# Two-layer convolution and attention kernel: order of first-image loads, idle matrix products, product order in q's first tile, and dealing of the sampling steps

## The chip, the cores and the metric

The kernel runs on one core of a Trainium2 chip, in one launch. The core has five engines that run their own instruction streams side by side: TensorE (PE; its weight loads are listed as PEld), VectorE (DVE), ScalarE (ACT), GpSimd (POOL) and SyncE (SP). They wait for each other through semaphores. Transfers between the chip's main memory and the on-chip buffers are issued here by SP's and POOL's queues and carried by 16 DMA engines. Matrix products are written to PSUM, a small memory of banks that DVE and ACT can read. The metric is device time in microseconds (us); the median of several runs counts.

## What is computed

Input x has 8 images of 512 channels and 64x64 pixels, in 32-bit floats. Two layers are added to it:

```
x = x + L0(group_norm(x))      # deformable attention
x = x + L1(group_norm(x))      # 1x1 conv, depthwise stride 2, two dense layers, depthwise deconv, 1x1 conv
```

Layer 0, cut to what matters here:

```
q    = w_q @ x                               # 512x512 times 512x4096, per image
t    = gelu(q[every 4th row and column] * w_off1 + b_off1)
off  = tanh(w_off2 @ t) * 4                  # 16x16 sampling points for each of 8 groups
kv_feats = bilinear_sample(q, grid + off)    # four neighbours of each point, weighted
k, v = split(w_kv @ kv_feats)
out  = softmax(q^T k / 8) v                  # 8 heads, 4096 queries, 256 keys
y    = w_out @ out + b_out
```

Group norm needs mean and variance of groups of 16 channels over the whole image, so no product of an image can begin before all of the image has been read and its statistic is done.

## The kernel before, in words

**Staging.** Images are worked one after the other. x of two images is held on chip. An image is 8 tiles (t = 0 to 7) of 512 pixels, each 128 partitions x 4 channel blocks x 512. All instructions stand in the order in which the code issues them (the schedule is by hand); each engine and each DMA queue keeps its own order.

**The first image.** At the top of the program two small arrays are loaded, `cst` (L114: the matrix that sums over groups, and constants of the sampling) and `vec` (L116: biases and small weights). Both stand on SP's queue ahead of `load_x(0)` (L1060, eight loads of 1 MB), `load_wq()` (the weights of q, in `wbuf`), `load_x(1)` and later weights. `norm_x` (L201) takes a statistic of each tile and channel block on DVE as it lands. `group_stats` joins them (L169), sums over groups with a product with `cst` (L173, tile `gps`), forms squared deviations on DVE, does a second such product (L182, `gpsb`), adds epsilon (L184) and takes the power -1/2 on POOL (L185). `norm_q` then normalises tile 0 on DVE and tile 1 on POOL (L217, four channel blocks each); later tiles are normalised on ACT (L221).

**q's seven products.** `project_q` computes a tile of q by a Winograd-Strassen scheme: seven products of quarter matrices instead of eight. `of_weights` and `of_tile` form the sums of weights (s1, s2, s4) and of pixels (t1, t2) on DVE: L253, L255, L257, L259 and L264, L266, L268, L270. `product` (L275) issues four matrix products of 128x128 by 128x256 in 32-bit floats; a trace shows two records for each, so a product is 8 records. In a tile, PE's order is: products 1 and 2, then 6 (s2, t2), 7, 5 (s1, t1), 4, 3. DVE adds them up as they come:

```
q12 = q11 + p6   (L364)      q11 += p2   (L365)      q22 = q12 + p7   (L372)
q12 += p5        (L378)      q21 = q22 + p4 (L385)   q22 += p5 (L386)   q12 += p3 (L391)
```

In tile 0, s4 is formed (L259) between L365 and L372, for all images but image 1, whose weights' sums are still there from image 0. Products 1 and 2 share a two-bank PSUM tile, and so do 7 and 4; products 6, 5 and 3 take single banks from a pool of two (`ps_mm`). From tile 1 on, transposes of the tile before (`by_pixel`, L324) stand between the products; tile 0 has none.

**Steps and dealing.** `project_q` is a generator; it yields a number for the PE work issued: 4, 2.5, 2.5, 2.5, 2.5 and 2 for the six parts of a tile, 16 together. `sample` is a generator too: it forms the sampling positions (three yields of 0), then goes through 20 slots (yield None). In them DVE computes row numbers (L516), POOL gathers q's pixels from main memory (L519), DVE weighs them (L483 to L488) and, twice, PE transposes the result (L493) into a bank of `ps_mm`, from where ACT copies it (L498). The sampling of image 0 is dealt among the q products of image 1 by the loop at L1087: each slot adds 6 units of room, and q steps are issued until the room is used up. When the slots are done, the rest of image 1's q follows. For later images other loops do this. Then `project_k` (L533) and `project_v` (L560) make k and v, and attention rounds begin, in which the next images' loads, statistics, q and layer 1 of the image before are mixed.

Of the kernel before, what the change touches and what calls it, by code (L numbers as in the profile page):

```python
# [8 lines left out]
F32 = mybir.dt.float32  # L9
# [7 lines left out]
P = 128  # L17
# [5 lines left out]
TP = 512  # L23
NT = N // TP
# [25 lines left out]
def kernel(  # L50
# [15 lines left out]
    nc = tc.nc  # L66
# [8 lines left out]
    ps_a = ctx.enter_context(tc.tile_pool(name="ps_a", bufs=1, space=PSUM))  # L75
# [20 lines left out]
    def spot(b, k):  # L96
        j = region[b]
        k %= NT + 1
        return spares[j] if k == 0 else regions[j][:, :, (k - 1) * TP : k * TP]

    def x_tile(b, t):
        return spot(b, t + 1)

    def q_tile(b, t):
        return spot(b, t)
# [5 lines left out]
    ident = cpool.tile([P, P], F32, name="ident")  # L111
    make_identity(nc, ident)
    cst = cpool.tile([P, K_N], F32, name="cst")
    nc.sync.dma_start(cst, consts)  # L114
    vec = cpool.tile([P, V_N], F32, name="vec")
    nc.sync.dma_start(vec, vecs)  # L116
    nhalf = cpool.tile([P, NCC], F32, name="nhalf")
    nc.vector.memset(nhalf, -0.5)

# [14 lines left out]
    def load_wq():  # L134
        nc.sync.dma_start(wbuf, w_qT.rearrange("(cc p) o -> p cc o", p=P))
# [19 lines left out]
    def drain(*gens):  # L155
        for gen in gens:
            for _ in gen:
                pass
# [35 lines left out]
    def load_x(b, order=range(NT), queue=nc.sync):  # L194
        for t in order:
            queue.dma_start(x_tile(b, t), xs[place[b]][:, :, t * TP : (t + 1) * TP])
# [7 lines left out]
    def quarters(a):  # L204

        h = C // 2
        return [[a[:, 2 * i : 2 * i + 2, h * j : h * (j + 1)] for j in range(2)] for i in range(2)]
# [25 lines left out]
    def project_q(b, normalise, mq, qd, pools, sums, aside=None):  # L233
# [8 lines left out]
        s1, s2, s4, t1, t2_, first = sums  # L242
# [29 lines left out]
        def product(bank, w, xh):  # L272
            for o in range(2):
                for k in range(2):
                    nc.tensor.matmul(  # L275
                        bank[:, o * 2 * P : (o + 1) * 2 * P],
                        w[:, k, o * P : (o + 1) * P],
                        xh[:, k, :],
                        start=(k == 0),
                        stop=(k == 1),  # L280
                    )
            return bank.rearrange("p (o n) -> p o n", o=2)
# [25 lines left out]
        def one_bank(t, n):  # L308
            return ps_mm.tile([P, TP], F32, tag="mm", name=f"pq_{b}_{t}_{n}")
# [33 lines left out]
        for t in range(NT):  # L343
            (x11, x12), (x21, x22) = quarters(x_tile(b, t))
            (q11, q12), (q21, q22) = quarters(q_tile(b, t))

            def pixels(k):

                if t:
                    by_pixel(t - 1, k)  # L350
                if t + 2 < NT:
                    normalise(t + 2, k)

            bank1, bank2 = two_banks(t, 0)
            p1 = product(bank1, w11, x11)
            p2 = product(bank2, w12, x21)
            nc.scalar.copy(q11, p1)
            of_tile(t, 4)
            if t:
                activate(t - 1)  # L360
            yield 4
            p6 = product(one_bank(t, 1), s2, t2_)
            pixels(0)
            V.tensor_add(q12, q11, p6)  # L364
            V.tensor_add(q11, q11, p2)  # L365
            if t == 0:
                of_weights(4)
            yield 2.5
            bank1, bank2 = two_banks(t, 2)
            p7 = product(bank1, w21, x12)  # L370
            pixels(1)
            V.tensor_add(q22, q12, p7)  # L372
            if aside and t in (3, 4):
                largest(2, t - 3)
            yield 2.5
            p5 = product(one_bank(t, 3), s1, t1)
            pixels(2)
            V.tensor_add(q12, q12, p5)  # L378
            if t + 1 < NT:
                of_tile(t + 1, 1)  # L380
                of_tile(t + 1, 2)
            yield 2.5
            p4 = product(bank2, w22, x21)
            pixels(3)
            V.tensor_add(q21, q22, p4)  # L385
            V.tensor_add(q22, q22, p5)  # L386
            if t + 1 < NT:
                of_tile(t + 1, 3)
            yield 2.5
            p3 = product(one_bank(t, 4), s4, x22)  # L390
            V.tensor_add(q12, q12, p3)  # L391
            if t == 2 and aside:
                aside()
            elif t + 1 < NT:
                largest(t, 0)
                largest(t, 1)
            yield 2
# [660 lines left out]

    with tc.manual_schedule():
        load_x(0)  # L1060
        load_wq()
        load_x(1)

        wkv = [es4[0:2], es4[2:4]]
        for i in range(2):
            for j in range(2):
                w = w_kvT.rearrange("(cc p) o -> p cc o", p=P)
                nc.sync.dma_start(wkv[i][j], w[:, 2 * j : 2 * j + 2, i * C : (i + 1) * C])
        load_weights_late()
        st = new_stats(0, 0)  # L1070
        drain(norm_x(0, st))

        shared = [wout[:, i, :].rearrange("p (k o) -> p k o", k=2) for i in range(3)]
        shared += [kt[:, 0:2, :], kt[:, 2:4, :], wout[:, 3, :]]
        drain(norm_q(0, st, norms))

        st = new_stats(0, 1)
        blocks, other = norm_x(1, st), norm_q(1, st, norms)
        for n, step in enumerate(make_q(0, shared)):
            if n >= 3 * NCC and next(blocks, "end") == "end" and n >= 10 * NCC:  # L1080
                next(other, None)
        drain(other)
        other = make_q(1, shared)
        next(other)
        rest.pop(0)()
        room = 0
        for step in samples[0]:  # L1087
            room += 6 if step is None else 2
            while room > 0:
                room -= next(other, 6) or 6  # L1090
        drain(other)
        rest.pop(1)()
        next(samples[1])
        load_wout()
        project_k(0, mqs.pop(0), wkv[0])
        logits(*names[0])
        project_v(0, wkv[1])
        for g in range(len(names) + LAG):
            b, r = divmod(g, ROUNDS)
            if r == 0 and b < B:  # L1100
                beside = next_image(b)
                st1s[b] = new_stats(1, b)

            def fill(room):
                while room > 0:
                    done = next(beside, None)
                    if done is None:
                        break
                    room -= done

            summed = g % 2 == 0 and 0 <= g - 1 < len(names)
            if g % 2 == 0:
                scale_two()
            if g < len(names):
                weighted_values(*names[g])
            if summed:
                sum_exps(*names[g - 1])
            if g < len(names):
                add_exps(*names[g])
            if r == Q_ROUND and 0 < b < B - 1:  # L1120

                tiles = [free_es.pop(0) for _ in range(3)]
                made = make_q(b + 1, room_for_sums(tiles), lambda: invert(*names[g - 1]))
                while next(made) != LATE:
                    pass
                free_es.extend(tiles)
                logits(*names[g + 1])
                drain(made)
                rest.pop(b + 1)()
            else:  # L1130
                if summed:
                    invert(*names[g - 1])
                if g + 1 < len(names):
                    logits(*names[g + 1])
            if g % 2:
                scale_two()
            phase[0] = 0
            if r >= LAG:
                fill(200)
            if g - LAG >= 0:  # L1140
                ob, ot, oc = names[g - LAG]
                project_out(ob, ot, oc, st1s[ob])
            k = g + 1 - LAG
            if 0 <= k < len(names) and k % NCC < 2:
                load_residual(*names[k + k % NCC], 2)
            if k >= NCC and k % NCC == 2 and names[k - NCC][0] < B - 1:
                store(*names[k - NCC][:2])
            phase[0] = 1
            if r >= LAG - 1:
                fill(200)  # L1150
            if b + 1 < B:
                if r == ROUNDS - 2:
                    drain(beside)
                    project_k(b + 1, mqs.pop(b + 1))
                if r == ROUNDS - 1:
                    project_v(b + 1)
        drain(layer1_last(B - 1, st1s.pop(B - 1), B - 2))
# [118 lines left out]
```

## Time and profile before

| | |
|---|---|
| median of 4 runs | 3288.21 us (3287.39 to 3289.61) |
| profiled execution | 3290.05 us |
| its span, first to last instruction | 3288.3 us |
| mean granted TensorE clock | 0.991 |
| DMA | 390.62 MB, mean 119 GB/s |

| line, engine | what | count | ns of one |
|---|---|---|---|
| L275 PE | products of q, 128x256 | 3584 records | 379 (median) |
| L560 PE | v, 128x512 | 16 in image 0 | 7.06 us from 283.89 on |
| L201 DVE | statistic of a block | 256 | 678 |
| L519 POOL | gather | 256 | 1109 |
| L217 DVE | normalise a block of tile 0, image 0 | 4 | 736 |

How to read it: the span counts from the first to the last instruction; the run's own time has some 1.8 us around it. A PE record's duration contains the filling of the array, so records overlap; the distance between starts says how fast PE works. A line of the timeline gives the start, the time to the end of the group, the engine, the line of the code, the operation, the tile written and those read, the shape, the count, and in brackets the idle time of that engine before it with what ended it.

### The profile page before, as it was taken

To read this page: it belongs to the slowest core of one execution; us is meant where nothing else is said; L and a number is where in the kernel's file an instruction comes from. 1 tells how busy PE (TensorE), PEld (TensorE's weight loads), DVE (VectorE), ACT (ScalarE), POOL (GpSimd) and SP (SyncE) were. 2 spreads that over 40 slices of the span, in tenths; PEclk is the share of its full clock that TensorE was granted. 3 is DMA by queue.
4 is the path that set the end of the run, shared out by engine and by line. 5 is a ranking of instruction groups with operands and counts; after the bars stand their busy time and mean duration, and the time that the engine had idled before them with its cause. 6 is when DMAs were issued, how large, how long until landed. Compare 5 with 4: busy or idle time off the path is not lost.

```text
span 3288.3 us, 46198 instructions
## 1 busy us (share of the span) xinstructions
PE 3207.1 (98%) x18196; PEld 1531.4 (47%) x18196; DVE 2330.1 (71%) x3786; ACT 1185.6 (36%) x1641; POOL 615.9 (19%) x576
## 2 busy tenths in 40 slices
PE   6999999999999999999999999999999999999996
PEld 5884223348332583326733276332853338533222
DVE  7884765787757777587765977668776687757565
ACT  2343333344323433344333443324432344333420
POOL 1130400130402304022030221303121040310201
PEclk9999999999999999999999999999999999999996
DMA  7232222672326623285332843248232582322713
GB/s 275 77 92 76 77 78 65 196 157 74 113 91 212 126 86 105 78 233 114 102 101 101 211 102 110 83 149 202 74 103 87 183 179 66 121 73 74 133 41 128
DMA packets 293874, 390.62 MB, mean 119 GB/s; under 512 B 18320, under 2 KB 157840, under 8 KB 293648
## 3 DMA queue, kind: packets, MB, share of 16 engines
q1 hardware_dynamic: 240368, 261.72, 24.4%
q0 software_dynamic: 53280, 125.86, 17.2%
q8 instruction: 145, 2.38, 0.3%
q14 instruction: 81, 0.66, 0.1%
HBM read 193.52 MB, written 192.94 MB: 118 GB/s over the span
## 4 chain that ended last, share of the span: by engine, by line
PE 93%; DVE 4%; issue 1%; ACT 1%; DMA 0%; SPq 0%; POOL 0%; ACTq 0%; DVEq 0%; POOLq 0%
PE pp L667 27%; PE pq L275 23%; PE ps L580 14%; PE pa L598 13%; PE pqt L324 4%; PE pn L625 4%; PE pk L533 2%; PE py L750 2%; PE pv L560 2%; PE po L893 2%; DVE rn L638 1%; PE po L424 0%; DVE st L201 0%; PE pu L848 0%; PE po_s L893 0%
## 5 line engine op out<-in xcount | busy, mean ns | idle before, releaser
L667 PE MATMUL pp<-image,wout 128*64 128x512 f32 x3584 | 820.2, 599 | 4.8 <-DVE image L653 4.6
L588 ACT ACTIVATE es<-ps 128x1024 f32<-128x1024 f32 x512 | 502.8, 1023 | 258.0 <-PE ps L580 208.7
L667 PEld LDWEIGHTS pp<-image,wout 128*64 128x64 f32 x3584 | 237.3, 137 | 549.7 <-issue 468.3
L598 PE MATMUL pa<-es,vt 128*64 128x512 f32 x2048 | 489.2, 598 | 1.7 <-ACT es L588 1.7
L519 POOL DMA_INDIRECT g<-qd,row x256 | 284.0, 1109 | 1053.9 <-DVE row L516 988.3
L275 PE MATMUL pq<-image,wbuf 128*128 128x256 f32 x2048 | 476.7, 381 | 3.3 <-DVE image L217 1.9
L580 PE MATMUL ps<-image,kt 64*64 64x512 f32 x3584 | 437.4, 602 | 0.3
L275 PEld LDWEIGHTS pq<-image,wbuf 128*128 128x128 f32 x2048 | 382.1, 191 | 56.2 <-issue 5.0
L674 DVE SCALAR_TENSOR_TENSOR image<-pp,vec,image 128x512 f32<-128x512 f32 x224 | 167.1, 746 | 335.9 <-PE pp L667 335.6
L605 ACT COPY image<-pa 128x512 f32<-128x512 f32 x224 | 132.1, 590 | 675.1 <-PE pa L598 675.1
L610 DVE TENSOR_TENSOR es<-es,es 128x1024 f32<-128x1024 f32 x256 | 310.8, 1214 | 71.4 <-PE pa L598 71.4
L598 PEld LDWEIGHTS pa<-es,vt 128*64 128x64 f32 x2048 | 137.4, 137 | 294.6 <-issue 274.8
L580 PEld LDWEIGHTS ps<-image,kt 64*64 64x64 f32 x3584 | 114.4, 132 | 307.7 <-issue 175.7
L638 DVE RECIPROCAL rn<-pn 128x512 f32<-128x512 f32 x64 | 214.6, 3353 | 7.7 <-PE pn L625 5.9
L334 ACT COPY qr<-pqt 128x512 f32<-128x512 f32 x224 | 131.2, 586 | 238.4 <-PE pqt L324 225.3
L185 POOL TENSOR_TENSOR gs<-ve,nhalf 128x4 f32<-128x4 f32 x16 | 16.7, 1042 | 1022.0 <-DVE ve L184 1022.0
L651 DVE STREAM_SHUFFLE rb<-rn 128x512 f32<-128x512 f32 x256 | 187.3, 732 | 0.1
L275 PE MATMUL pq<-es,es 128*128 128x256 f32 x768 | 181.5, 379 | 0.0
L945 POOL DMA_DIRECT2D out_dram<-part x126 | 138.1, 1323 | 153.8 <-ACT part L940 146.5
L201 DVE BATCH_NORM_STATS2 st<-image 128x6 f32<-128x512 f32 x256 | 159.2, 678 | 7.5 <-DMA image<-in_x_dram 7.4
L677 DVE BATCH_NORM_STATS2 st<-image 128x6 f32<-128x512 f32 x224 | 155.6, 694 | 7.7
L653 DVE TENSOR_TENSOR image<-image,rb 128x512 f32<-128x512 f32 x224 | 155.0, 692 | 7.8
(197 smaller groups left out, 3491.4 us busy)
## 6 DMA issues: line engine op xcount, KB each, us to landing
qd<-qr SPq DMA_DIRECT2D x256, 256.0 KB
image<-in_x_dram SPq DMA_DIRECT2D x112, 512.0 KB
out_dram<-image SPq DMA_DIRECT2D x49, 1024.0 KB
image<-in_x_dram POOLq DMA_DIRECT2D x48, 1024.0 KB, 10.6
out_dram<-part POOLq DMA_DIRECT2D x126, 256.0 KB, 7.1
image<-in_x_dram SPq DMA_DIRECT2D x16, 1024.0 KB
wbuf<-in_w_kvT_dram SPq DMA_DIRECT2D x14, 1024.0 KB
out_dram<-spare POOLq DMA_DIRECT2D x56, 256.0 KB, 8.0
```

What stands on the lines that cost most here:

```text
L201: nc.vector.bn_stats(st[:, cc, t, :], x_tile(b, t)[:, cc, :])
L275: nc.tensor.matmul(bank[:, o * 2 * P : (o + 1) * 2 * P], w[:, k, o * P : (o + 1) * P], xh[:, k, :], start=(k == 0), stop=(k == 1),)
L519: nc.gpsimd.indirect_dma_start(held[-1][:, i, :, :].rearrange("p j d -> p (j d)"), None, qd[:, :], bass.IndirectOffsetOnAxis(ap=row[:, ky, ...
L580: nc.tensor.matmul(ps[k : k + DH, a, :], kt[r : r + DH, hp, kc * P + k : kc * P + k + DH], qt[r : r + DH, hp, :], start=True, stop=True,)
L588: nc.scalar.activation(e, ps, AF.Exp)
L598: nc.tensor.matmul(pa[a * DH : (a + 1) * DH, :], vt[:, kc, hd * DH : (hd + 1) * DH], es[kc][:, a, :], start=(kc == 0), stop=(kc == 1),)
L610: nc.vector.tensor_add(es[0], es[0], es[1])
L638: nc.vector.reciprocal(rn, denominators.pop((b, t)))
L651: nc.vector.stream_shuffle(rb, rn, [2 * (hp % 2) + hp // 2] * 32)
L667: nc.tensor.matmul(pp[r : r + DH, :], wout[:, hp, oc * P + r : oc * P + r + DH], ao[:, hp, :], start=(hp == 0), stop=(hp == NCC - 1),)
L674: nc.vector.scalar_tensor_tensor(xt[:, oc, :], pp, col(V_BOUT + oc), xt[:, oc, :], ALU.add, ALU.add)
L677: nc.vector.bn_stats(st[:, oc, t, :], xt[:, oc, :])
```

## The change

Four edits:

- `cst` and `vec` are issued after `load_x(0)` instead of at the top.
- Five matrix products whose result nobody reads, of the unit matrix with 512 pixels of x's tile 6, are put between the statistic's DVE work and its first sum over groups; two more between its second sum and the first product of q. They write a PSUM bank that is first used later.
- In tile 0 of every image, product 5 is issued before product 6, third after 1 and 2. The additions keep their order.
- In the loop that deals image 0's sampling among image 1's q, a slot adds 4.5 units of room instead of 6.

```diff
@@ top
     cst = cpool.tile([P, K_N], F32, name="cst")
-    nc.sync.dma_start(cst, consts)
     vec = cpool.tile([P, V_N], F32, name="vec")
-    nc.sync.dma_start(vec, vecs)
@@ project_q, in the loop over tiles
             yield 4
+            if t == 0:
+                p5 = product(one_bank(t, 3), s1, t1)
             p6 = product(one_bank(t, 1), s2, t2_)
             pixels(0)
             V.tensor_add(q12, q11, p6)
@@
             yield 2.5
-            p5 = product(one_bank(t, 3), s1, t1)
+            if t:
+                p5 = product(one_bank(t, 3), s1, t1)
             pixels(2)
             V.tensor_add(q12, q12, p5)
@@ main part
         load_x(0)
+        nc.sync.dma_start(cst, consts)
+        nc.sync.dma_start(vec, vecs)
         load_wq()
         load_x(1)
@@
+        idle = ps_a.tile([P, TP], F32, tag="pa", name="idle")
+        for _ in range(5):
+            nc.tensor.matmul(idle, ident, x_tile(0, NT - 2)[:, 0, :], start=True, stop=True)
         drain(norm_q(0, st, norms))
+        for _ in range(2):
+            nc.tensor.matmul(idle, ident, x_tile(0, NT - 2)[:, 0, :], start=True, stop=True)
@@
         for step in samples[0]:
-            room += 6 if step is None else 2
+            room += 4.5 if step is None else 2
```

The code has the idle products of the second group after `drain(norm_q(...))`, so in PE's stream they stand between `gpsb` and the first product of q.

## The prediction

> **What bounds the kernel now.** I read the page's first part, then a table of stages made with the windows view, then the timeline of the first 50 us, of images 1 and 2, and the waits of TensorE (PE).
>
> ```profile
> span 3288.3 us, 46198 instructions
> ...
> PE 3207.1 (98%) x18196; PEld 1531.4 (47%) x18196; DVE 2330.1 (71%) x3786; ACT 1185.6 (36%) x1641; POOL 615.9 (19%) x576
> ```
>
> ```profile
> 0.00:48.10 48.10, 15.52 (x61) 13.15 (x62) 35.60 (x69) 4.69 (x6) 12.28 (x11) 1.00 0.99 362
> ...
> 141.00:272.70 131.70, 125.50 (x663) 111.57 (x662) 101.71 (x185) 45.56 (x75) 41.55 (x37) 1.00 0.32 90
> ...
> 717.10:3190.00 2472.90, 2470.19 (x14126) 1163.78 (x14124) 1765.16 (x2841) 927.36 (x1280) 470.64 (x443) 1.00 0.42 117
> ```
>
> The second table's columns are the stretch, its length, then busy us of PE, weight loads, DVE, ACT and POOL, the granted clock, the DMA share and GB/s. From image 2 on, PE is busy for 2470.19 of 2472.90 us: whatever delays PE there is paid in full, and nothing later can absorb it. Idle PE time that can be won lies in the first 48 us (32.6) and beside image 1's q (6.2).
>
> The timeline of the first stage (start, us, engine, line):
>
> ```profile
> 0.75 0.41 SPq L114 DMA_DIRECT2D cst<-in_consts_dram  x1
> 1.68 13.08 SPq L196 DMA_DIRECT2D image<-in_x_dram  x8
> 23.59 2.48 DVE L201 BATCH_NORM_STATS2 st<-image 128x6 f32<-128x512 f32 x4 [0.24 <-DMA image<-in_x_dram]
> 26.30 2.47 DVE L201 BATCH_NORM_STATS2 st<-image 128x6 f32<-128x512 f32 x4 [0.24 <-DMA image<-in_x_dram]
> 29.79 0.59 PE L173 MATMUL gps<-mv,cst 128*128 128x4 f32 x2 [29.79 <-DVE mv L169]
> 33.76 5.86 PE L275 MATMUL pq<-image,wbuf 128*128 128x256 f32 x16 [1.94 <-DVE image L217]
> ```
>
> DVE waits 0.24 us for each tile of x, every 2.71 us: the transfer sets the start. The 16 records of the first two products then take 5.70 us (33.76 to 39.46), though 16 take 3.45 later: single records start 0.427 us apart until about 38.2 and 0.216 after. PE is slow for its first 4.4 us of work; the granted-clock column shows 1.00 and doesn't tell it.
>
> Tile 0 of image 2, where PE has no gap:
>
> ```profile
> 722.41 1.89 PE L275 MATMUL pq<-image,wbuf 128*128 128x256 f32 x8
> 722.67 0.69 DVE L364 TENSOR_TENSOR spare<-spare,pq 128x512 f32<-128x512 f32 x1 [1.09 <-PE pq L275]
> 723.39 0.69 DVE L365 TENSOR_TENSOR spare<-spare,pq 128x512 f32<-128x512 f32 x1
> 723.99 0.69 DVE L259 TENSOR_TENSOR es<-wbuf,es 128x512 f32<-128x512 f32 x1
> 724.14 1.89 PE L275 MATMUL pq<-es,es 128*128 128x256 f32 x8
> 724.59 0.68 DVE L372 TENSOR_TENSOR spare<-spare,pq 128x512 f32<-128x512 f32 x1
> 725.86 1.89 PE L275 MATMUL pq<-image,wbuf 128*128 128x256 f32 x8
> ```
>
> Products 7, 5 and 4 start at 722.41, 724.14 and 725.86, 1.73 apart. Product 4 (L383) shares a two-bank PSUM tile with product 7, and the built program makes it wait for L372, which reads product 7. L372 ends at 725.27; product 5 covers that wait. That the wait is real shows in image 1, where DVE was late:
>
> ```profile
> 162.60 1.99 PE L275 MATMUL pq<-image,wbuf 128*128 128x256 f32 x8 [1.33 <-DVE spare L372]
> ```
>
> **The change, part by part.** Lines are those of before.
>
> *Product 5 third in tile 0, images 2 to 7.* The order becomes 1, 2, 5, 6, 7, 4, 3; DVE's order stays. No product is added, and 5 has its inputs (L264 ends at 718.5). Now 7 stands directly before 4. In image 2: product 5 takes 6's place at 720.68, 6 starts at 722.41, 7 at 724.14 and ends at 725.86. L364 starts 1.99 after 6's start, as now (720.68 to 722.67): 724.40; L365 0.72 later, L259 0.60, L372 0.60: 726.32; its 0.68 and 0.04 to PE (145.97 to 146.01 at L386) give 727.04. Product 4 waits 1.18 us, and behind it in PE's queue product 3 and all that follows. The six images show these rows alike to 0.01 us: 6 x 1.18 = **+7.08**. Cover lost, nothing gained there: PE had no gap between 2 and 6.
>
> *Image 1's tile 0.* Two products end at 154.15, the sample's small products at 155.85, then 5, 6 (157.66), 7 (159.38, ends 161.11). L364 at 159.64 instead of 158.93, so L365, the eight position instructions and L372 come 0.71 later, and so does product 4: **+0.71**.
>
> *Constants behind x.* x is issued 0.93 us sooner (1.68 against 0.75), so all tiles land up to 0.93 sooner. Bounds: 0, if the ramp of the first transfers doesn't move; 1.21 with 106.5 KB at 387 GB/s beside it. I take 0.93, the issue row. On SP's queue cst and vec are moved past eight loads and, by the program, wait for x's first two tiles; behind them stand the q weights and image 1's loads. cst lands after the last tile (25.4) and its own 1.0 us (1.8 to 2.8 now), 26.4, against its use at 28.86; the weights 2.7 later, 29.1, against 32.5; vec is first used at 53.6, image 1's x at 66.3. All covered; if cst's cover went, the statistic would slip by what is missing.
>
> *Five idle products.* Each is two records of 512 columns: 0.441 us fast (L560: 16 in 7.06) and 0.854 slow (twice 0.427). They start when tile 6 lands, 23.59 - 0.93 = 22.66. With 4.4 us slow, as at 33.76, 5.15 records are slow and 4.85 fast: end 29.20. The statistic's product stands behind them and is ready at 28.86: 0.34 late. Bounds: all fast 27.07, no delay; all slow 31.20, 2.34 late. I take 4.4, since the second slow stretch (272.73 to about 277) has the same length. gps and gpsb then take 0.28 instead of 0.59, as in image 1 (at 141.93 and 144.35): -0.62. L217 starts at 33.16 - 0.93 + 0.34 - 0.62 = 31.95.
>
> *Two idle products* go from 30.60 to 32.36, in the gap before 32.55 (L217 + 0.60): free if fast; slow they would end at 34.02. PE's gaps here are under 1 us; gaps of 1.06 and 1.33 at 222 and 162 didn't slow what followed, 5 us with only transposes and 4-column products (267.7 to 272.7) did.
>
> The Trainium skill ("TensorE: Matmul & The Clock Gate", Part 1: The HAM clock gate) says that the clock is released after a busy window of about 3.4 us that runs freely, so the slow stretch lasts 3.4 to 6.8 us and differs from run to run. By it the idle products end between 28.7 and 30.4, and image 0's gain below would be 2.2 to 0.7 us.
>
> *Tile 0 of image 0.* Products 1 and 2, now fast, are paced by L217's quarters (0.68 each) and end at 36.33 (39.46 now). t1 (L264, 37.55 - 1.21 = 36.34) lets product 5 start at 36.38; 6 at 38.11, 7 at 39.84 to 41.57. L364 at 40.10, L365 40.82, L259 41.42, L372 42.02 to 42.70; product 4 at 42.74, 3 at 44.47, tile 1 at 46.20 against 48.09: **-1.89**, with the same wait before 4 inside. Without the move, 6 would wait for L266 (37.54) and tile 1 would start within 0.1 of that. Bounds: -2.23 without delay; +2.6 if PE stays slow throughout.
>
> *Samples dealt at 4.5 instead of 6.* It moves image 0's sampling ahead inside image 1's q. Two stalls come from the transposes of the samples (L493), which take a PSUM bank that product 3 then lacks:
>
> ```profile
> 222.29 1.99 PE L275 MATMUL pq<-image,wout 128*128 128x256 f32 x8 [1.06 <-DVE image L386]
> 265.66 1.99 PE L275 MATMUL pq<-image,wout 128*128 128x256 f32 x8 [0.77 <-ACT image L498]
> ```
>
> Product 3 could have started at 221.09 (220.62 + 0.47) and 264.76: 1.20 and 0.90 lost. In the new program they stand before product 4 of tile 3 (its bank already free; product 3 then waits for the copy L498, some 2.0 us after the transposes' predecessor, with 2.67 of PE work to cover it) and behind product 3 of tile 5. **-2.10**. Bounds: 0 (stalls only moved) and -2.10. DVE: 10.0 us of q work a tile plus 1.78 gathers of 1.33 is 12.8 of 13.96. A gather lands 2.4 to 3.4 us after its issue; it now has 7.85 us (9 of 16 units of a tile), before 10.5. Covered; if not, DVE blocks and PE behind it.
>
> **Sum**: 7.08 + 0.71 - 1.89 - 2.10 = **+3.80**. The profiled execution took 3290.05 us around its span of 3288.3, 1.84 above the median of 3288.21. Its span becomes 3292.1; on the median: **3292.0 us**. Under 0.2% (6.6 us) can't be told from no change here; +3.80 is 0.12%.
>
> **Rivals.**
> - *The wait before product 4 costs nothing.* Then 0 for images 1 to 7's tile 0, and -3.06 in image 0: -5.16, 3283.0 us. For it: only that banks differ. Against: the row at 162.60.
> - *Idle products hold up the statistic* (slower). If PE is still slow at 31.2, the statistic waits 2.34, tile 0 runs slow and image 0 costs +2.6 instead of -1.89: 3296.5. It crosses 0.2% once image 0 loses 0.9. For: ten records of 0.854 don't fit ahead of 28.86. Against: the one measured ramp ended after 4.4.
> - *Denser samples only move the stalls* (the gain of 2.10 falls away): 3294.1. For: DVE has 1.1 us left in a tile. Against: the banks named above.
> - *The change doesn't do what it says*, product 5 filling a gap in image 0 alone: without the 7.79 it would be 3284.2; but the condition is on the tile, not on the image.
>
> **How the numbers follow.** Forecast 0.62, wait free 0.08, late statistic 0.13, stalls moved 0.13, else 0.04. The range 3289.0 to 3295.6 holds the first and the fourth, and part of the others (a free wait in some images, a partly late statistic). Faster by 0.2% (below 3281.6) needs more than all gains together: 0.03. Slower (above 3294.8): the late statistic and the edge of the fourth, 0.15. Within: 0.82.
>
> **What would show it.** In images 2 to 7 a wait of PE's product 4 on L372 of about 1.2 us, once each; L217 starting near 31.95; the first two products at 0.216 a record; tile 1 at 46.2; no stalls at the samples' transposes. A PE without waits in 717 to 3190 would prove the largest term wrong.

## The result and the profile after

| | before | after |
|---|---|---|
| median | 3288.96 us (60 runs) | 3293.64 us (40 runs) |
| lowest to highest | 3285.88 to 3291.60 | 3291.41 to 3295.68 |
| profiled execution | 3290.05 | 3293.67 |
| its span | 3288.3 | 3291.8 |

The change costs 4.7 us: the ratio is 1.0014, 95% interval 1.0009 to 1.0018. That is clear of chance over so many runs, and below the 0.2% that the prediction calls no change. 3292.0 was forecast, with 3289.0 to 3295.6 as range.

The page of after, first part, and the windows view with the same stretches as before (stretch, length, then busy us of PE, weight loads, DVE, ACT and POOL, granted clock, DMA share, GB/s):

```profile
span 3291.8 us, 46214 instructions
...
PE 3213.9 (98%) x18210; PEld 1532.3 (47%) x18210; DVE 2330.7 (71%) x3786; ACT 1185.3 (36%) x1641; POOL 614.8 (19%) x576
```

```profile
0.00:48.10 48.10, 23.35 (x82) 15.91 (x83) 37.72 (x72) 4.70 (x6) 12.28 (x11) 1.00 1.00 366
...
717.10:3190.00 2472.90, 2464.08 (x14086) 1158.72 (x14086) 1760.80 (x2831) 927.00 (x1280) 468.07 (x443) 1.00 0.42 117
```

The idle products take 8.5 us of PE's busy time in the first 48 us, and the row of products 1 and 2 is 1.7 shorter (4.12, before 5.86); together that is about the page's 6.8 us more. In the steady stretch PE had 2.7 us without work; it now has 8.8.

The timeline of after, first stage (start, us, engine, line, tiles, count; in brackets the idle time before and what ended it). Lines have moved: L215 is before's L217, L273 its L275, L372 is still L372.

```profile
22.61 6.57 PE L1081 MATMUL idle<-image,ident 128*128 128x512 f32 x10 [22.61 <-DMA image<-in_x_dram]
...
29.02 0.28 PE L171 MATMUL gps<-mv,cst 128*128 128x4 f32 x2
...
31.87 2.71 DVE L215 TENSOR_SCALAR image<-image,gs 128x512 f32<-128x512 f32 x4 [1.14 <-POOL gs L183]
...
32.47 4.12 PE L273 MATMUL pq<-image,wbuf 128*128 128x256 f32 x16
...
36.43 3.62 PE L273 MATMUL pq<-kt,wout 128*128 128x256 f32 x16
...
42.82 1.99 PE L273 MATMUL pq<-image,wbuf 128*128 128x256 f32 x8 [1.05 <-DVE spare L372]
```

Products 1 and 2 take 3.96 us to the start of product 5 (before, 5.70 to that of product 6). Sixteen records alone would take 3.45; PE pauses once among them, until 33.30, for L215's second block. Products 5 and 6 follow without a gap, and product 4 waits for L372. Tile 1 starts at 46.38; it was 48.09.

Tile 0 of image 2 in the same view, and PE's waits from 50 to 3190 us (us in all, times, longest):

```profile
716.84 3.62 PE L273 MATMUL pq<-es,es 128*128 128x256 f32 x16
720.29 1.89 PE L273 MATMUL pq<-image,wbuf 128*128 128x256 f32 x8
723.21 1.99 PE L273 MATMUL pq<-image,wbuf 128*128 128x256 f32 x8 [1.03 <-DVE spare L372]
725.04 1.89 PE L273 MATMUL pq<-image,es 128*128 128x256 f32 x8
```

```profile
PE pq L273 <- DVE spare L372: 8.6, 7, 2.1
```

The same view of before:

```profile
PE pq L275 <- DVE spare L372: 1.3, 1, 1.3
```

Product 7 starts at 720.29 and 4 at 723.21: 2.92 instead of 1.73. The wait stands once in each of images 1 to 7; the seven make 8.6 us, where before had one of 1.3, in image 1. The number in brackets (1.03) is less than what is lost (1.19), because records overlap: a product's row is 1.89 long, and the next product normally starts 1.73 after it.

The two stalls are gone. Product 3 of tiles 4 and 7 of image 1's q, before at 222.29 and 265.66 with waits of 1.06 and 0.77, follows its predecessor without one:

```profile
219.76 1.89 PE L273 MATMUL pq<-image,wout 128*128 128x256 f32 x8
...
262.11 1.89 PE L273 MATMUL pq<-image,wout 128*128 128x256 f32 x8
```

Read stage by stage, from the starts of records in the two traces:

| stage | before | after | difference | forecast |
|---|---|---|---|---|
| to tile 1 of image 0 | 48.09 | 46.38 | -1.71 | -1.89 |
| to tile 1 of image 1 | 118.07 | 118.81 | +0.74 | +0.71 |
| to k (first record of `pk`) | 106.57 | 103.88 | -2.69 | -2.10 |
| to image 2's q | 444.39 | 444.21 | -0.18 | 0 |
| to the end | 2571.16 | 2578.53 | +7.37 | +7.08 |
| span | 3288.28 | 3291.81 | +3.53 | +3.80 |

### The profile page after: what moved, and what is told of

It is laid out like the page before. It is cut to its first block, busy times and chain, and to the rows that moved or that the text cites. A ratio compares the mean times of both kernels' runs of the same rounds, so it can differ in the third digit from the quotient of the medians.

```text
span 3291.8 us, 46214 instructions
## 1 busy us (share of the span) xinstructions
PE 3213.9 (98%) x18210; PEld 1532.3 (47%) x18210; DVE 2330.7 (71%) x3786; ACT 1185.3 (36%) x1641; POOL 614.8 (19%) x576
## 4 chain that ended last, share of the span: by engine, by line
PE 94%; DVE 4%; issue 1%; ACT 0%; DMA 0%; SPq 0%; POOL 0%; DVEq 0%; ACTq 0%; POOLq 0%
PE pp L668 27%; PE pq L273 23%; PE ps L581 14%; PE pa L599 13%; PE pqt L322 4%; PE pn L626 4%; PE pk L534 2%; PE py L751 2%; PE pv L561 2%; PE po L894 2%; DVE rn L639 1%; PE po L425 0%; PE pu L849 0%; DVE st L199 0%; PE po_s L894 0%
## 5 line engine op out<-in xcount | busy, mean ns | idle before, releaser
L273 PE MATMUL pq<-image,wbuf 128*128 128x256 f32 x2048 | 475.5, 380 | 9.9 <-DVE spare L372 9.7
L273 PEld LDWEIGHTS pq<-image,wbuf 128*128 128x128 f32 x2048 | 380.0, 191 | 65.5 <-DVE spare L372 12.9
L273 PE MATMUL pq<-es,es 128*128 128x256 f32 x768 | 180.5, 379 | 0.0
## 6 DMA issues: line engine op xcount, KB each, us to landing
image<-in_x_dram POOLq DMA_DIRECT2D x48, 1024.0 KB, 10.1
```

The costliest lines, as they stand in the source:

```text
L273: nc.tensor.matmul(bank[:, o * 2 * P : (o + 1) * 2 * P], w[:, k, o * P : (o + 1) * P], xh[:, k, :], start=(k == 0), stop=(k == 1),)
```

## Experiments

Twelve further kernels ran, each beside the kernel before on the same chip. The kernel before had medians of 3288.6 to 3289.2 there.

**Product 5 back in fifth place**

```diff
-            if t == 0:
-                p5 = product(one_bank(t, 3), s1, t1)
             p6 = product(one_bank(t, 1), s2, t2_)
@@
-            if t:
-                p5 = product(one_bank(t, 3), s1, t1)
+            p5 = product(one_bank(t, 3), s1, t1)
```

> The changed kernel with product 5 back in fifth place in tile 0; the other three edits stay. Theory (product 4 waits for the reader of product 7): the six waits of images 2 to 7 go (in the trace of the changed kernel tile 0 takes 13.48 there instead of 12.20, once 13.84: 8.1 us together), image 1's tile 0 gains 0.75, and image 0's tile 0 gains some 0.2 (product 6 would start at 37.5, tile 1 at 46.15 instead of 46.38): 9.1 us less than the changed kernel, 3284.6 us, 4.3 below the kernel before. Rival (the move is what speeds image 0's tile 0): image 0 loses 1.7 and the run is at 3286.5. Rival (the longer stretch from image 2 on is not product 5's): little change, 3293.

Measured 3285.05 us, ratio to before 0.9986 (0.9977 to 0.9995). The windows view of this kernel:

```profile
717.10:3190.00 2472.90, 2470.29 (x14126) 1161.36 (x14125) 1762.57 (x2835) 927.66 (x1281) 470.50 (x443) 1.00 0.43 117
```

PE's busy time is back at before's 2470.2. Tile 0 takes 12.19 in images 2 to 7, as before, and image 0's tile 1 starts at 46.46, as fast as with the move. So without the move the change is faster than before, and the move gave image 0 nothing that could be measured.

**Product 5 moved, and nothing else** (on the kernel before)

```diff
+            if t == 0:
+                p5 = product(one_bank(t, 3), s1, t1)
             p6 = product(one_bank(t, 1), s2, t2_)
@@
-            p5 = product(one_bank(t, 3), s1, t1)
+            if t:
+                p5 = product(one_bank(t, 3), s1, t1)
```

> The kernel before with product 5 third in tile 0 as its only edit. Theory: 8.1 us in images 2 to 7, 0.75 in image 1, 1.27 in image 0 (product 4 waits until 45.81 where it started at 44.64, and the restart costs 0.1): 10.1 us above the kernel before, 3299.0 us. Rival (the wait appears only together with the other edits): no more than 1 us above the kernel before.

Measured 3296.15 us, 1.0023 (1.0013 to 1.0033). Slower by 7.0, less than the 10.1 expected. In its trace tile 0 takes 13.49 in all six images (expected), image 0 loses 1.89 and image 1 2.43 (more than expected), and later stretches are shorter than before's, among them k (9.72 us from `pk` to `pv`; 11.09 before). Image 1's excess and the shorter k go with PE's slow windows, below: the trace's clock record has one at 165.65 and none at k. From the last image's q to the end it took only 0.2 more than before, though a wait of 1.29 stands there too; why was not found.

**Product 4 in a bank of its own.** Product 5 stays third. Product 4 takes the bank that L364 has emptied, product 3 the second bank of 7's tile.

```diff
+            bank6 = one_bank(t, 1)
             if t == 0:
                 p5 = product(one_bank(t, 3), s1, t1)
-            p6 = product(one_bank(t, 1), s2, t2_)
+            p6 = product(bank6, s2, t2_)
@@
-            p4 = product(bank2, w22, x21)
+            p4 = product(bank2 if t else one_bank(t, 4), w22, x21)
@@
-            p3 = product(one_bank(t, 4), s4, x22)
+            p3 = product(one_bank(t, 4) if t else bank2, s4, x22)
```

> The changed kernel, in whose tile 0 product 4 goes into a single bank (the one that product 6 leaves when L364 has read it) and product 3 into the second bank of product 7's tile. Product 5 stays third; no instruction is added. Theory (the wait comes from the PSUM tile that 4 shares with 7): product 4 starts 1.73 after 7 in all images, product 3 finds L372 done; images 2 to 7 gain 8.1, image 1 up to 1.8 (product 3 waits for L372 there), image 0 1.2: 11 us less than the changed kernel, 3282.5 us, 6.4 below the kernel before. Rival (DVE is simply behind and PE would wait for it at the next place): the wait turns up at product 3 or in tile 1, and the run is at 3291 to 3294.

Measured 3284.29 us, 0.9986 (0.9977 to 0.9995): 9.4 below the changed kernel with the same order of products. Its timeline in image 2 and in image 0:

```profile
714.82 3.62 PE L273 MATMUL pq<-es,es 128*128 128x256 f32 x16
718.27 3.62 PE L273 MATMUL pq<-image,wbuf 128*128 128x256 f32 x16
721.73 1.89 PE L273 MATMUL pq<-image,es 128*128 128x256 f32 x8
```

```profile
22.58 7.52 PE L1082 MATMUL idle<-image,ident 128*128 128x512 f32 x10 [22.58 <-DMA image<-in_x_dram]
29.93 0.28 PE L171 MATMUL gps<-mv,cst 128*128 128x4 f32 x2
```

Products 7 and 4 are one run of 16 records: the wait is gone from images 2 to 7, without a change of DVE's order. That shows its cause: the PSUM tile that 4 shared with 7. Image 1 gained 1.7 of the 1.8 expected up to its tile 1 (117.07 instead of 118.81), but DVE is late there, and 1.56 came back before k (105.44 instead of 103.88), all of it in tile 2, which took 15.53 instead of 13.97: in that image the rival holds. With image 0's gain smaller too, 9.4 us were won instead of 11. And the idle products, the same as in after, here ended so late that the statistic's product waited from 28.61, when its input was ready, to 29.93.

**Constants first again**

```diff
+    nc.sync.dma_start(cst, consts)
...
+    nc.sync.dma_start(vec, vecs)
...
         load_x(0)
-        nc.sync.dma_start(cst, consts)
-        nc.sync.dma_start(vec, vecs)
```

> The changed kernel with the two constant arrays loaded at the top again, ahead of x. Theory (x's arrival sets the statistic): x lands 1.0 later, all of it reaches tile 1: 3294.6 us. Rival (x's start is hidden by the transfer or by the idle products): no change, 3293.6.

Measured 3294.67 us, 1.0019 (1.0010 to 1.0028), 1.0 above the changed kernel. The statistic's input was ready at 29.64 instead of 28.63, tile 1 started at 47.55 instead of 46.38. In the trace the move of the constants is thus worth 1.0 us at the statistic, about its issue time (0.93); the medians' 1.0 alone is within the scatter.

**Room of 6 in the dealing**, in the changed kernel, **and room of 4.5 alone**, in the kernel before

```diff
-            room += 4.5 if step is None else 2
+            room += 6 if step is None else 2
```

> The changed kernel with 6 units of room for each slot instead of 4.5. Theory (the denser dealing moves two transposes to where the bank is free): the two stalls come back, 1.20 and 0.90 as in the kernel before or the 2.7 that the two traces differ by in image 1's q after tile 0: 3295.7 to 3296.3 us. Rival (stalls only moved): within 0.5 of the changed kernel.

> The kernel before with 4.5 units of room for each slot instead of 6 as its only edit. Theory (the two stalls at the samples' transposes go, and nothing takes their place): from tile 1 of image 1 to k the traces with 4.5 take 103.88 us and those with 6 take 106.24 to 106.57, so 2.4 to 2.7 less: 3286.5 us. Rival (the gain in this stage comes back later, since the median of the changed kernel with 6 units was only about 1 us higher): 3288 to 3289.

In the traces both did what was expected: from tile 1 of image 1 to k it is 106.24 with 6, and 103.87 with 4.5 alone. The medians show less: 3294.59 (1.0018, 1.0009 to 1.0027), 1.0 above the changed kernel, and 3287.58 (0.9995, 0.9986 to 1.0004), 1.6 below before and no difference that could be told. The trace with 6 shows where the rest went in that execution: against after's, image 1's tile 0 takes 1.7 more and k 1.7 less, as PE's slow windows (below) fall elsewhere, and the stretch from image 2's q to the end is 1.2 shorter, so that the span is only 1.0 longer. Whether that is so in other executions was not settled.

**No idle products**

```diff
-        idle = ps_a.tile([P, TP], F32, tag="pa", name="idle")
-        for _ in range(5):
...
-        for _ in range(2):
...
```

> The changed kernel without its seven idle products. Theory (they pay the slow first 4.4 us of PE): the statistic's sums slow again, so that L215 starts near 32.1, the first two products take 5.7 us instead of 3.9, product 4 of image 0's tile 0 starts near 44.7 instead of 42.82: 1.9 us above the changed kernel, 3295.5 us. Rival (x's arrival alone sets image 0): no change, 3293.6. Rival (they hold up the statistic): faster than the changed kernel.

Measured 3297.08 us, 1.0020 (1.0011 to 1.0029), 3.4 above the changed kernel. Two surprises stand in its trace. Products 1 and 2 took 6.53 us, 0.8 more than in the kernel before. The timeline of this kernel, and that of the kernel before with room 4.5, which has no idle products either:

```profile
32.65 6.69 PE L273 MATMUL pq<-image,wbuf 128*128 128x256 f32 x16 [1.94 <-DVE image L215]
```

```profile
33.73 5.17 PE L275 MATMUL pq<-image,wbuf 128*128 128x256 f32 x16 [1.95 <-DVE image L217]
```

The same products, 6.7 us here and 5.2 there. And in image 1, products 4 and 3 after the wait of 2.1 took 5.25 instead of 3.55. The windows view of the kernel without idle products around them:

```profile
161.60:165.00 3.40, 1.32 (x7) 0.85 (x6) 3.06 (x14) 0.00 (x0) 0.00 (x0) 1.00 0.00 0
165.00:168.40 3.40, 3.40 (x10) 2.68 (x9) 3.16 (x15) 0.00 (x0) 0.00 (x0) 0.50 0.00 0
```

PE worked 1.32 of 3.40 us, and for the next 3.40 its granted clock was 0.50. In the trace's clock record every stretch at 0.50 is one or more pieces of 3.41 us (the last one is cut off by the end), all on one grid through the whole execution, and the grid lies elsewhere in each execution. Laid over the first stage (times in us; "fast from" is the first record at full pace):

```
                      PE at work   window it falls into     next window      fast from
without idle (e3)     32.65        31.87-35.28  77% used    35.28-38.70      38.74
own bank              22.58        21.77-25.18  76%         25.18-28.60      28.65
after                 22.61        19.90-23.32  21%         23.32-26.73      26.87
before                33.76        31.30-34.71  43%         34.71-38.12      38.16
room 6                22.61        22.06-25.47  84%                          25.5
room 4.5 alone        33.73        33.30-36.71  87%                          36.80
```

In these six, PE becomes fast at the end of the first window in which it worked 84% or more; 77% was not enough. The slow stretch so lasted 2.9 to 6.1 us, by chance of phase. The busy share is not the whole rule, though. In six of the fourteen traces, after's and before's among them, a window around k's start, used to 92%, mostly by transposes and products with 4 columns, was followed by one at 0.50. From after:

```profile
265.66:269.07 3.41, 3.13 (x26) 2.85 (x25) 1.52 (x3) 0.20 (x1) 0.00 (x0) 1.00 0.53 154
269.07:272.49 3.42, 3.42 (x8) 2.52 (x8) 3.23 (x4) 0.00 (x0) 0.00 (x0) 0.50 0.69 165
```

The share counts the modelled lengths of records, and short products start 0.11 to 0.12 apart with lengths of 0.25 to 0.28, so it may overstate their work; no run separates that. And at 0.50, a window used to 92% could be followed by another slow one, as the next experiment shows.

**Three idle products instead of five; no second group**

```diff
-        for _ in range(5):
+        for _ in range(3):
```

> The changed kernel with three idle products in the first group instead of five. If PE becomes fast after some 4.4 us of work, the three end at 25.2 still slow (6 records of 0.427), PE idles until 28.6, and the products of q start slow again or become fast within them: tile 1 of image 0 starts 0.5 to 1.9 later than 46.38, 3294.1 to 3295.5 us. If PE becomes fast a fixed time after its first work, idle or not, nothing changes: 3293.6.

```diff
-        for _ in range(2):
-            nc.tensor.matmul(idle, ident, x_tile(0, NT - 2)[:, 0, :], start=True, stop=True)
```

> The changed kernel without the second group of two idle products. PE then works only 0.7 us (the two sums of the statistic) between 29.2 and 32.5. If so short a gap leaves PE fast: no change, 3293.6 us, first two products of q in 3.9 us. If it makes PE slow again: they take 5.7, and the run is 1.9 later, 3295.5.

Measured 3293.92 us (1.0016, 1.0007 to 1.0025) and 3294.23 us (1.0017, 1.0008 to 1.0027): 0.3 and 0.6 above the changed kernel, too little to tell. (The first expectation took 0.427 for a record of 512 columns; slow, it takes 0.85, so the three products end at 27.4.) Their timelines, the one with three first:

```profile
28.89 0.38 PE L171 MATMUL gps<-mv,cst 128*128 128x4 f32 x2 [1.47 <-DVE mv L167]
30.11 0.59 PE L180 MATMUL gpsb<-dv,cst 128*128 128x4 f32 x2 [0.84 <-DVE dv L177]
30.56 3.76 PE L1084 MATMUL idle<-image,ident 128*128 128x512 f32 x4
34.12 4.89 PE L273 MATMUL pq<-image,wbuf 128*128 128x256 f32 x16
```

```profile
32.36 5.74 PE L273 MATMUL pq<-image,wbuf 128*128 128x256 f32 x16 [1.94 <-DVE image L215]
```

With three, the window 26.44 to 29.85 was 40% used, and PE was slow from 29.85 to 36.68: the two later idle products took 3.6 us instead of 1.8, and the first product of q waited behind them until 34.12. The windows on this trace's grid show that one used to 92% (3.15 of 3.41) did not end the slow stretch:

```profile
26.44:29.85 3.41, 1.36 (x5) 0.44 (x3) 2.86 (x10) 0.00 (x0) 0.00 (x0) 1.00 1.05 387
29.85:33.26 3.41, 3.15 (x5) 1.60 (x6) 1.55 (x5) 0.00 (x0) 2.17 (x2) 0.50 1.05 387
33.26:36.68 3.42, 3.42 (x9) 2.36 (x8) 3.42 (x7) 0.00 (x0) 3.42 (x2) 0.50 1.05 387
```

In layer 1 of before's last image, too, windows used to 98, 100 and 100% (3260.31 to 3270.55) passed at 0.50, and the clock rose only after the next.

Without the second group the window 29.69 to 33.10 was a third used, and products 1 and 2 were slow again. In after, 26.73 to 30.14 was 75% used, and PE stayed fast. In these two traces tile 1 starts 2.4 and 1.5 later than in after, which the medians do not show. In the second, the stretch from k to image 2's q is 1.8 shorter than in after and makes up for it; how often other executions meet that phase was not measured.

**Idle products sooner and more** (on the kernel with product 4 in its own bank)

```diff
-        for _ in range(5):
-            nc.tensor.matmul(idle, ident, x_tile(0, NT - 2)[:, 0, :], start=True, stop=True)
+        for _ in range(7):
+            nc.tensor.matmul(idle, ident, x_tile(0, NT - 3)[:, 0, :], start=True, stop=True)
```

> The kernel with product 4 in a bank of its own, with seven idle products that need tile 5 of x instead of five that need tile 6, so that they begin 2.7 us sooner, near 19.9. Theory (PE works at half pace until the end of the first whole window of 3.41 us, on a fixed grid, in which it was busy; that is 3.4 to 6.8 us after it starts): the fast pace is reached by 26.7 at the latest, the idle products end between 27.6 and 29.3, and the statistic's product, ready at 28.6, waits 0 to 0.7 where it waited 1.3 in the trace of the kernel without this edit; the median falls by 0.5 to 1 us, to 3283.5. Rival (idle products that run longer delay the statistic more): no change or slower.

Measured 3283.68 us, 0.9982 (0.9973 to 0.9991), 0.6 below the kernel without this edit, no more than the scatter. The statistic no longer waited (28.79), but its last idle product ended near 27.9, the window 27.04 to 30.45 was 53% used (1.82 of 3.41), and the next ran at 0.50: tile 1 at 45.84, against 45.98.

**Idle products in the last image's layer 1, and at 319 us** (on the kernel with product 4 in its own bank; `keep_busy` is n products of the unit matrix into a free bank, `fill_gap` the same in the last image alone; the comments are put in here)

```diff
+        fill_gap(2)      # before L752's products; likewise 3 and 1 before the two sums
...
+        fill_gap(6)      # before pz; then one narrow one before ph, pht and pu
...
+        fill_gap(4)      # behind pu
...
+                if (ob, ot, oc) == (0, 0, 0):
+                    keep_busy(ident, 12, P)
```

> The kernel with product 4 in a bank of its own, with idle products in the gaps of PE in the last image's layer 1 (after 3185 us) and in the wait of the first output product of image 0 (at 319). Theory (a window of 3.41 us with little work on PE halves PE's pace in the next): the half-pace window at 322 goes (1.7 us), the 64 records of L752 in layer 1 take 6.9 us instead of 9.3, the small products and the output products after them run at full pace where PE, not DVE, sets it: 5 to 8 us less, 3277 to 3279 us. Rival (the idle products hold up what stands behind them, or DVE sets the end of layer 1 anyway): no more than 2 us less, or slower.

Measured 3282.11 us, 0.9980 (0.9971 to 0.9989), only 2.2 less. The trace has both halves of it. From image 7's q to the end it takes 574.4 us instead of 579.8, a gain of 5.4. But the products meant for the wait at 319 stood behind the product that waits, not inside it, ran slow for 2.94 us and held up attention; the stretch from k to image 2's q became 2.9 longer. The half-pace window there stayed (319.49 to 322.90 in this trace's clock record), since the products did not fill the wait.

**All together**: product 4 in its own bank, the earlier idle products and two narrow ones between the statistic's sums, ten narrow ones inside the product that waits at 319, those of layer 1, and three behind its first six output products. Beyond the edits shown:

```diff
@@ group_stats, ahead of the second sum
+        if which == 0 and b == 0:
+            keep_busy(x_tile(0, NT - 3)[:, 0, :], 2, 2 * P)
@@ project_out, in the loop over hp
+            if (b, t, oc, hp) == (0, 0, 0, 2):
+                keep_busy(ident, 10, P)
@@ project_last
+                if len(todo) == 26 and b == B - 1:
+                    keep_busy(out_tile(b - 1, 0)[:, 0, :], 3)
```

> The kernel with product 4 in a bank of its own and idle products wherever a trace showed PE slow after a gap: seven that need tile 5 of x, two narrow ones between the two sums of the first statistic, ten narrow ones inside the first output product of image 0 (in its wait of 2.6 us, where the kernel with idle products in layer 1 had them behind that product and lost 2.9), those in the last image's layer 1, and three after the first six output products there. Theory (windows of 3.41 us): the half-pace windows at 30, 320 and 3251 go; 0.8 in image 0, 1.9 at 320, 5.4 in layer 1 (579.8 to 574.4 from image 7's q to the end in the two traces) and 1 to 2 more at its end: 3284.3 - 9 to 10 = 3274 to 3275.5 us. Rival (no more than the gains already seen, DVE sets layer 1's end and the narrow products delay the statistic): 3279.

Measured 3274.87 us, 0.9960 (0.9946 to 0.9973): 13.7 below the kernel before in the same call, 18.8 below the changed kernel's median. The windows view of layer 1, first the kernel with only product 4 moved, then this one:

```profile
3222.00:3232.00 10.00, 9.54 (x96) 2.76 (x96) 0.44 (x3) 0.82 (x2) 0.04 (x1) 0.76 0.01 2
3232.00:3250.00 18.00, 5.96 (x54) 3.15 (x54) 10.71 (x32) 0.72 (x2) 0.00 (x0) 0.64 0.00 0
```

```profile
3222.00:3232.00 10.00, 9.50 (x84) 3.60 (x72) 5.24 (x13) 1.18 (x2) 0.00 (x0) 1.00 0.00 0
3232.00:3250.00 18.00, 16.13 (x96) 7.41 (x98) 13.48 (x34) 2.35 (x4) 2.40 (x2) 1.00 0.17 62
```

The clock was 0.76 and 0.64 and is 1.00; the work there is done sooner, so the stretch now holds later work too. In the clock record two stretches at 0.50 are left, one window at 3199.8 and the last 13 us.

## Why the prediction was right, point by point

- *Product 4 waits for the reader of product 7, six times 1.18.* Shown: undoing the move takes 8.6 us off the median with image 0 and 1 included, and moving only the bank takes the wait away with the order unchanged. Each wait cost 1.29: 1.19 ahead of product 4, where the working has 1.18, and 0.10 in the step from product 4 to 3 (1.83 instead of 1.73), which it left out. Image 5 paid 1.64; why stays open. The six tiles 0 so grew by 8.1. That the whole stretch from image 2's q on grew by only 7.37, near the 7.08 forecast, is luck: other parts of it were 0.8 shorter in this pair of traces. From image 7's q to the end it grew by 0.9 instead of 1.3, but three kernels with the old order (before, product 5 back, 4.5 alone) already differ there by 1.0 (579.3 to 580.3).
- *Image 1, +0.71.* 0.74 in this pair of traces. In three others with the same order a slow window fell there and it was 2.43.
- *Image 0, -1.89.* -1.71. x came 1.0 sooner (0.93 taken, from the issue row); the statistic's product waited 0.39 for the idle products (0.34 taken); L215 began at 31.87 (31.95), product 4 at 42.82 (42.74). The size was right for this execution, and the working's slow stretch of 4.4 us was one draw out of 2.9 to 6.1: where it lasted 6.0, the statistic waited 1.3. Its second support was misread: in before's k the records from 272.73 to 273.74 still start 0.22 to 0.32 apart, and the piece at 0.50 lies from 273.64 to 277.06, 3.4 us and not 4.4. So the rival "idle products hold up the statistic" isn't another case but the end of one scatter.
- *Dealing, -2.10.* -2.69 in the stage. 2.36 of it stands at the two places that were named, and is what the changed kernels with 6 and 4.5 differ by (106.24 and 103.88); the other 0.33 is a pause in tile 3 of before's trace (2.52 us from product 4 to 3 instead of 2.19) that the kernel with room 6 does not have. The stalls did not move on. On the medians it shows as 1.0 and 1.6, so this term is confirmed in the traces alone. The working's sum for DVE does not come out: 10.0 and 1.78 times 1.33 are 12.4, not 12.8, so 1.6 us are left in a tile; the forecast does not use it.
- *The wait is free.* False: it is there seven times. *The change does not do what it says.* False: the condition on the tile acts in every image.
- *The sum on the median.* +3.80 forecast, +3.53 in the span of the one pair of traces, +4.68 on the medians. Before's traced execution (3290.05) lay 1.1 above its median of 60 runs, the changed kernel's (3293.67) at its own; 3.53 and 1.1 make the 4.6 to 4.7. The forecast took before's terms from that one execution and set the sum on the median as if they were the same. In the absolute figures, 3292.0 against 3293.64, another 0.75 of the 1.6 is the starting point: the four runs that the forecast had gave 3288.21, the sixty 3288.96. Where the 1.1 lies was not found: slow windows, as in k (9.72 us from `pk` to `pv` in eight traces, 11.1 to 11.4 in six, both kernels' among these), come and go between executions.

Of the rule from the Trainium skill ("TensorE: Matmul & The Clock Gate", Part 1: The HAM clock gate) that was weighed in the prediction, the runs agree with the free-running window of about 3.4 us: the pieces are 3.41 long. They differ from the bounds of 3.4 to 6.8 us that the prediction worked out from it: 2.9 to 6.1 us were measured (the shortest in the kernel with room 6, whose first window was 84% used).

## What to carry over

Before a product is put earlier because its inputs are ready, look at what its old place covered: the two products that become neighbours may share a PSUM tile, and on a saturated engine that wait is paid in each repetition, while the gap that the move was meant to fill stood in image 0 alone. Giving one of them another bank cost nothing here and showed the cause at once. Idle products pay (9.4 us here, all places together) where PE pauses in a stage that PE sets, if they fill the pause without standing ahead of work that is ready; a product in a wrong place of the queue costs its whole length.

## What was not expected of the hardware

- The clock of PE is granted in windows of 3.41 us on a grid whose phase differs from execution to execution. In the first 170 us, windows used to 32 to 40% and one used to 53% were followed by one at 0.50; others used to 48, 53 and 75% were not. No bound on the share fits all: around k's start, windows used to 92%, mostly by transposes and 4-column products, were followed by one at 0.50 in six traces. At 0.50, records of 128x256 start 0.427 us apart instead of 0.216.
- The same code therefore differs by some 1.3 us in one stage: tile 1 of image 0 starts at 45.98 in the kernel with product 4 in its own bank and at 44.69 in the one that differs from it only after 315 us.
- At the start of an execution the clock column says 1.00 while the records are 0.427 apart (32.65 to 38.70 in the kernel without idle products). The clock record's first entry begins only at 38.70, so the distance of the records is what to read there.
